# Three sets of four token tiles of the FFN's second layer as seven quarter products each; gates computed beside the first layer

## The chip, the cores and the metric

The kernel runs on one core of a Trainium2 chip. The metric is the time of one execution on the device in microseconds; 273.91 us is the median of 3 runs (273.66 to 274.04). All views below come from one execution, recorded by the hardware profiler (273.66 us).

The engines are named as the profile names them: PE (matrix products; PEld is its loading of the stationary operand), DVE (element-wise work), ACT (activations and copies out of PSUM), POOL (here the gathers and scatters of rows) and SP (which issues the loads of matrices). SBUF is the on-chip memory; PSUM holds the results of PE[...].

## The reference

Everything is fp32. There are 2048 tokens (4 x 512) of width 512.

```python
# first part: one of four experts for each token, chosen by its id
g = silu(einsum('bsd,fd->bsf', hidden_states, Wg[e]))      # Wg = Wu = Wd = ctx_2048
u = einsum('bsd,fd->bsf', hidden_states, Wu[e])
y = einsum('bsf,df->bsd', g * u, Wd[e])
out = where((expert_ids == e)[..., None], y, out)
x = x + tanh(g_xattn[0]) * out                             # hidden_states = layernorm(x)

# second part: a dense FFN, whose result is summed into 8 rows
route_probs = softmax(xr @ wr.T)                           # xr = layernorm(x)
routes_k, indices_k = top_k(route_probs, 2)
gates = routes_k / sum(routes_k)
h = silu(xr @ w1.T)
h = silu(h @ w3.T)
h = h @ w2.T
for k in range(2):
    out = out.at[indices_k[:, k]].add(gates[:, k:k+1] * h) # indices 0..7 are row numbers
x = x + tanh(g_ffn[0]) * out
```

The indices of the second part are row numbers of the output, so only rows 0 to 7 receive anything from the FFN. The kernel therefore sums the gated activations of all tokens into 8 rows before it multiplies by w2.

## The kernel before

The tokens are sorted by expert into 17 passes of 128 rows. A loop runs over the passes in a fixed `order`; iteration `i` issues, for different passes, `up` (product with the expert's matrix, line 537 or 522, into `z`), `turn_in`, `centre`, `look_at`, `gather`, `down` (second product, line 522, into `y`; line 571 adds it to the row), `load_free` (the next expert matrices), `turn_out` (transposed normed rows into `hT2`), `norms`, and then one or two `step()`s of the FFN. The order on each engine is the order in which the program issues (there is no scheduler): an instruction that waits holds up everything issued behind it on its engine.

The FFN works on two blocks `b` of 1024 tokens. `hT2[b]` holds a block's normed tokens, `s1` the first layer's output: 4 chunks of 128 features by 1024 tokens, of which columns 0 to 511 are "half 0" and 512 to 1023 "half 1". `ffn(b)` is a generator, and each `step()` runs it to its next `yield`. Block 0 starts in iteration 10 and its steps lie between the passes of iterations 11 to 18; block 1 starts in iteration 18 and has the chip to itself.

`first_layer` (lines 699 to 784) already forms the product with w1 by seven quarter products for eight (a 2 x 2 block product after Strassen and Winograd): products p1 to p7 out of sums `S1..S4` of quarters of w1 and `T1..T4` of quarters of `hT2`. X is a PSUM tile into which p1, p6, p5 and p3 are added one after the other, read in between by ACT (`kept`) or DVE (`active`).

`second_layer` forms the product with w3 in the plain way: `gated(t)` takes a tile of 128 tokens, four products of 128 x 128 by 128 x 512 into the PSUM tile `v` (line 824), and a Silu into `s2` (line 832). For each half of a block, 4 tiles; 16 in all. The very last tile is made in two halves of 256 columns. Then `add` multiplies `s2` by the gates `g` and sums it into four 32-row groups of `acc` (line 836); `pay` issues the adds of the half before. `route` (lines 623 to 667) finds the two largest logits and the gates on DVE, with one Tanh on ACT; it is issued in one piece ahead of each half's tiles.

Expert matrices are tiles of 1 MB in a pool of `MP = 7` buffers. `load_free` issues the load of unit `n` once the pass that last used unit `n - MP` has been issued in full:

```python
        while n < len(units) and (
            n < MP or max(order.index(p) for p in units[n - MP][0]) < i
        ):
            n += 1
```

A unit is one expert matrix; a pass with rows of all four experts has four of them, and neighbouring whole passes share one. Loads leave on SP's queue in the order of issue, w1, w3 and w2 among them. PSUM is divided into pools: `ps_mm` (2 banks: `z`, `y`, `Z`, `v`), `ps_x` (2: the logits and X), `ps_y` (1: Y), `ps_tp` (2: transposes), and one for `acc`. A tile of a pool takes over the bank of the second last one of that pool, and its first product waits until that one has been read.

Of the kernel before, what the change touches and what calls it, by code (L numbers as in the profile page):

```python
# [8 lines left out]
F32 = mybir.dt.float32  # L9
# [4 lines left out]
AF = mybir.ActivationFunctionType  # L14
# [5 lines left out]
P = 128  # L20
# [5 lines left out]
def tile_gated_moe_ffn(  # L26
# [45 lines left out]
    nc = tc.nc  # L72
# [15 lines left out]
    assert NB == 2 and KC == 4  # L88

    const = ctx.enter_context(tc.tile_pool(name="const", bufs=1))  # L90
    MP = 7
    mp = ctx.enter_context(tc.tile_pool(name="mp", bufs=MP))
    xp = ctx.enter_context(tc.tile_pool(name="xp", bufs=6))
    work = ctx.enter_context(tc.tile_pool(name="work", bufs=3))
# [528 lines left out]
    def route(b, lt):  # L623

        def st(name, shape=(P, TT, NR)):
            return small.tile(list(shape), F32, tag=name, name=f"{name}_{b}")

        def wide(a):
            return a.unsqueeze(2).to_broadcast([P, TT, NR])

        def first_max(src, i):
            mx = st(f"mx{i}", (P, TT))
            nc.vector.tensor_reduce(mx, src, AX.X, ALU.max)  # L640
            oh = st(f"oh{i}")
            nc.vector.tensor_tensor(oh, src, wide(mx), ALU.is_equal)
            nc.vector.tensor_mul(oh, oh, rank)
            rk = st(f"rk{i}", (P, TT))
            nc.vector.tensor_reduce(rk, oh, AX.X, ALU.max)
            nc.vector.tensor_tensor(oh, oh, wide(rk), ALU.is_equal)
            return mx, oh

        l1 = lt[:, :, 0:NR]
        m1, oh1 = first_max(l1, 1)  # L650
        l2 = st("l2")
        nc.vector.scalar_tensor_tensor(l2, oh1, -1e30, l1, ALU.mult, ALU.add)
        m2, oh2 = first_max(l2, 2)
        d = st("d", (P, TT))
        nc.vector.tensor_sub(d, m1, m2)
        half = st("half", (P, TT))
        nc.scalar.activation(half, d, AF.Tanh, scale=0.5)
        p1 = st("p1", (P, TT))
        nc.vector.tensor_scalar(p1, half, 0.5, 0.5, ALU.mult, ALU.add)
        p2 = st("p2", (P, TT))  # L660
        nc.vector.tensor_scalar(p2, half, -0.5, 0.5, ALU.mult, ALU.add)
        g = small.tile([P, TT, Q], F32, tag="g", bufs=2, name=f"g_{b}")
        nc.gpsimd.memset(g, 0.0)
        nc.vector.tensor_tensor(oh1, oh1, wide(p1), ALU.mult)
        nc.vector.tensor_tensor(oh2, oh2, wide(p2), ALU.mult)
        nc.vector.tensor_add(g[:, :, 0:NR], oh1, oh2)
        return g

    def sums_of_w1():

        h = D // 2
        a11, a12 = w1[:, 0:2, 0:h], w1[:, 2:4, 0:h]
        a21, a22 = w1[:, 0:2, h:D], w1[:, 2:4, h:D]
        ss = [ffp.tile([P, 2, h], F32, tag=f"S{i}", name=f"S{i}") for i in range(1, 5)]
        w1_sums.extend((a11, a12, a22, ss))
        nc.vector.tensor_add(ss[0], a21, a22)
        yield
        nc.vector.tensor_sub(ss[1], ss[0], a11)
        yield
        nc.vector.tensor_sub(ss[2], a11, a21)  # L680
        yield
        nc.vector.tensor_sub(ss[3], a12, ss[1])
        yield

    def sums_of_hT(b):


        lgs = [logits(b, half) for half in range(2)]
        b11, b12 = hT2[b][:, 0:2, 0:HB], hT2[b][:, 0:2, HB:TB]
        b21, b22 = hT2[b][:, 2:4, 0:HB], hT2[b][:, 2:4, HB:TB]  # L690
        ts = [ffp.tile([P, 2, HB], F32, tag=f"T{i}", name=f"T{i}_{b}") for i in range(1, 5)]
        nc.vector.tensor_sub(ts[0], b12, b11)
        lts[b] = [turned(b, half, lg) for half, lg in enumerate(lgs)]
        nc.vector.tensor_sub(ts[1], b22, ts[0])
        nc.vector.tensor_sub(ts[2], b22, b12)
        nc.vector.tensor_sub(ts[3], b21, ts[1])
        return b11, b21, b22, ts
# [108 lines left out]

    def ffn(b):

        yield from first_layer(b)
        for half in range(2):  # L810
            yield from second_layer(2 * b + half, route(2 * b + half, lts[b][half]))

    NH = 2 * NB

    def second_layer(b, g):

        c_b = b % 2 * HB

        def gated(t, half=None):

            c0, n = (0, D) if half is None else (half * D // 2, D // 2)
            v = ps_mm.tile([P, n], F32, tag="mm", name=f"v_{b}_{t}_{c0}")
            for k in range(KC):
                nc.tensor.matmul(  # L824
                    v,
                    s1[:, k, c_b + t * P : c_b + (t + 1) * P],
                    w3[:, k, c0 : c0 + n],
                    start=(k == 0),
                    stop=(k == KC - 1),
                )  # L830
            s2 = work.tile([P, n], F32, tag="s2", bufs=5, name=f"s2_{b}_{t}_{c0}")
            nc.scalar.activation(s2, v, AF.Silu)  # L832
            return s2

        def add(t, s2):
            nc.tensor.matmul(  # L836
                acc[t * Q : (t + 1) * Q, :],
                g[:, t, :],
                s2,
                start=(b == 0),  # L840
                stop=(b == NH - 1 if t < TT - 2 else b == NH - 2),
            )

        def pay():

            for f, t, s2 in owed:
                f(t, s2)
            owed.clear()

        def add_turned(t, k, s2):  # L850

            nc.tensor.matmul(  # L852
                accT[:, k, :],
                s2,
                g[:, t, 0:NR],
                start=(t == TT - 2 and k == 0),
                stop=(t == TT - 1 and k == KC - 1),
                skip_group_check=True,
            )

        s2s = []
        if b < NH - 1:
            for t in range(TT):
                s2s.append(gated(t))
                if t == 0:
                    pay()
                yield
            owed.extend((add, t, s2s[t]) for t in range(TT))
            return
        for t in range(TT - 1):  # L870
            s2s.append(gated(t))
            if t == 0:
                pay()
            yield
        for t in range(TT - 2):
            add(t, s2s[t])
        a = work.tile([P, D], F32, tag="g", bufs=1, name="a")
        nc.scalar.copy(a, acc)
        half0 = gated(TT - 1, 0)
        for k in range(KC):  # L880
            add_turned(TT - 2, k, s2s[TT - 2][:, k * P : (k + 1) * P])
        tp = transposed(a, "sum")
        nc.vector.tensor_reduce(
            aT[:, :, 0:NR],
            tp.rearrange("p (k t q) -> p k q t", k=KC, t=TT)[:, :, 0:NR, :],
            AX.X,
            ALU.add,
        )
        def finish(i, s2):
            n = KC // 2  # L890
            for k in range(n):
                add_turned(TT - 1, i * n + k, s2[:, k * P : (k + 1) * P])
            ks = slice(i * n, (i + 1) * n)
            nc.vector.tensor_add(aT[:, ks, 0:NR], aT[:, ks, 0:NR], accT[:, ks, :])

        finish(0, half0)
        half1 = gated(TT - 1, 1)
        out_product(0, KC // 2)
        finish(1, half1)

    o = []
# [15 lines left out]

    SHORT = 1
    last = {b: max(i for i, p in enumerate(order) if min(p // (TB // P), NB - 1) == b) for b in range(NB)}
    running, hT_sums, lts, w1_sums = [], {}, {}, []  # L920

    def step():
        if running:
# [52 lines left out]
    turn_mid(order[1])  # L976
    norms(order[4], order[0])
    summing = sums_of_w1()
    owed = []
    for i in range(2, NP + 2):  # L980
        if i < NP:
            up(order[i])
        if i + 1 < NP:
            turn_in(order[i + 1])
        if i + 2 < NP:
            centre(order[i + 2])
        if i + 3 < NP:
            look_at(order[i + 3])
        if i + 4 < NP:
            gather(order[i + 4])  # L990
        if i <= NP:
            down(order[i - 1])
        load_free(i)
        turn_out(order[i - 2])
        if i <= NP:
            norms(order[i + 3] if i + 3 < NP else None, order[i - 1])
        step()
        if i > NP:
            step()
        if 6 <= i < 10:  # L1000
            next(summing)
        if i == 4:
            w1 = load_w(w1T, "w1")
            wr = load_w(wrT, "wr")
        if i == 8:
            w3 = load_w(w3T, "w3")
        if i == 12:
            w2 = load_w(w2T, "w2")
        if i < NP:
            turn_mid(order[i])  # L1010
        for b in range(NB):
            if last[b] == i - 2:
                hT_sums[b] = sums_of_hT(b)
                running.append(ffn(b))
        if last[0] != i - 2:
            step()
# [53 lines left out]
```

## Time and profile before

| what | value |
|---|---|
| median of 3 runs (lowest, highest) | 273.91 us (273.66, 274.04) |
| profiled execution: its time | 273.66 us |
| profiled execution: span from first to last instruction | 271.9 us |
| PE busy | 264.2 us, 1383 products |
| DVE, ACT, POOL busy | 146.5, 63.5, 39.1 us |
| granted clock of PE, mean | 0.997 |
| line 824 (`v`) on the chain that ended last | 20% of the span |
| bytes moved | 37.32 MB, mean 137 GB/s |

The span leaves out 1.76 us of the profiled execution's time, which lie around it. An fp32 product of the program appears as two loads of the stationary operand and two MATMUL records, so one tile of `gated` is 8 records. Records overlap (each is longer than the distance to the next), so what a product costs is read from the distance between starts or from the chain of waits, not from the mean length of a record. The chain of waits lists, in order of time, what had to end before the next thing could start; a line of it is the start, the length, the engine and the tile.

### The profile page before, as it was taken

The page shows a single profiled execution, that of the slowest core. Times are in us where ns is not written, and L with a number is a line of the kernel's source. Part 1 is how long each engine was busy: PE and PEld are TensorE (multiplying, and loading weights), DVE is VectorE, ACT ScalarE, POOL GpSimd, SP SyncE. Part 2 cuts the span into 40 slices and gives each one's busy share as a digit, 9 for nine tenths or more (in the row PEclk, how much of TensorE's full clock was granted, in tenths as well). Part 3 has the DMA queues.
Part 4 walks back from the last instruction along what each step waited for, and adds up shares of the span by engine and source line. Part 5 has one row for each costly group of instructions (what it writes and reads, how often), then busy time and mean ns, then how long its engine had stood idle before and what let it go on. Part 6 is the DMA issues. An engine that isn't in the chain of part 4 may idle for free.

```text
span 271.9 us, 3831 instructions
## 1 busy us (share of the span) xinstructions
PE 264.2 (97%) x1383; PEld 142.2 (52%) x1383; DVE 146.5 (54%) x498; ACT 63.5 (23%) x124; POOL 39.1 (14%) x61
## 2 busy tenths in 40 slices
PE   5999999999999999999999999999999999999994
PEld 2545484757783757435746534464445444344363
DVE  6697986864888989936263471417244521701000
ACT  2013232122222121233041231211122233301120
POOL 5440122211222320311010100101010000000000
PEclk9999999999999999999999999999999999999998
DMA  0666994499974459915429510100010000000000
GB/s 1 236 193 257 387 393 172 140 303 377 367 275 168 155 155 375 350 42 162 185 75 386 194 39 2 39 0 10 2 41 0 0 2 0 0 0 0 0 2 4
DMA packets 18083, 37.32 MB, mean 137 GB/s; under 512 B 2063, under 2 KB 2127, under 8 KB 18064
## 3 DMA queue, kind: packets, MB, share of 16 engines
q1 hardware_dynamic: 15312, 28.41, 29.6%
q0 software_dynamic: 2720, 8.65, 8.8%
q8 instruction: 11, 0.18, 0.3%
q14 instruction: 8, 0.07, 0.1%
q10 hardware_dynamic: 32, 0.01, 0.0%
HBM read 32.86 MB, written 4.47 MB: 137 GB/s over the span
## 4 chain that ended last, share of the span: by engine, by line
PE 96%; DMA 2%; DVE 1%; issue 0%; DVEq 0%
PE y L522 22%; PE v L824 20%; PE z L537 13%; PE X L716 10%; PE z L522 9%; PE Y L716 5%; PE tp_f L407 3%; PE tp_a L407 3%; PE Z L716 3%; PE idle L212 2%; PE acc L836 1%; PE lg L793 1%; DMA x<-in_x_dram,from_row 1%; PE tp_g L407 1%; PE accT L852 1%; DMA idt<-in_ids_dram 1%
## 5 line engine op out<-in xcount | busy, mean ns | idle before, releaser
L824 PE MATMUL v<-w,s 128*128 128x512 f32 (+1 forms) x136 | 57.2, 570 | 0.0
L824 PEld LDWEIGHTS v<-w,s 128*128 128x128 f32 x136 | 25.1, 190 | 28.2 <-issue 27.1
L537 PEld LDWEIGHTS z<-hT,m 128*128 128x128 f32 x320 | 36.8, 192 | 1.6 <-issue 1.4
L537 PE MATMUL z<-hT,m 128*128 128x128 f32 x320 | 37.5, 275 | 0.0
L522 PE MATMUL y<-m,g 128*128 128x512 f32 x80 | 36.1, 594 | 0.0
L572 POOL DMA_INDIRECT out_dram<-x,to_row x17 | 17.2, 1009 | 90.8 <-DVE x L571 89.0
L522 PE MATMUL z<-m,hT 128*32 128x512 f32 (+1 forms) x152 | 25.7, 596 | 0.6 <-DVE hT L471 0.6
L522 PE MATMUL y<-m,gT 128*32 128x512 f32 (+1 forms) x152 | 25.4, 595 | 0.0
L418 POOL DMA_INDIRECT x<-in_x_dram,rows_on x14 | 14.4, 1027 | 63.0 <-DVE x L571 19.6
L522 PEld LDWEIGHTS y<-m,g 128*128 128x128 f32 x80 | 14.4, 190 | 15.2 <-issue 15.2
L571 DVE SCALAR_TENSOR_TENSOR x<-y,tg,x 128x512 f32<-128x512 f32 x17 | 12.6, 740 | 17.7 <-PE y L522 17.7
L555 DVE TENSOR_TENSOR g<-z,g 128x512 f32<-128x512 f32 x14 | 9.6, 688 | 22.0 <-ACT g L554 22.0
L554 ACT ACTIVATE g<-z 128x512 f32<-128x512 f32 x14 | 8.4, 598 | 48.3 <-PE z L537 36.1
L832 ACT ACTIVATE s<-v 128x512 f32<-128x512 f32 (+1 forms) x17 | 9.7, 571 | 42.2 <-PE v L824 42.2
L609 ACT COPY hT<-tp_f 128x512 f32<-128x512 f32 x13 | 7.6, 586 | 39.9 <-PE tp_f L407 39.9
L372 DVE BATCH_NORM_STATS2 st_a<-x 128x6 f32<-128x512 f32 x17 | 11.7, 686 | 6.6 <-DMA x<-in_x_dram,rows_on 6.6
L522 PEld LDWEIGHTS z<-m,hT 128*32 128x32 f32 (+1 forms) x152 | 7.9, 122 | 13.8 <-issue 10.6
L716 PE MATMUL X<-T,S 128*128 128x512 f32 x32 | 15.0, 592 | 0.0
L522 PEld LDWEIGHTS y<-m,gT 128*32 128x32 f32 (+1 forms) x152 | 8.1, 122 | 12.1 <-issue 12.0
L407 PEld LDWEIGHTS tp_f<-ident,h_f 128*128 128x128 f32 x68 | 8.2, 141 | 10.2 <-issue 10.2
L372 DVE BATCH_NORM_STATS2 st_f<-x 128x6 f32<-128x512 f32 x17 | 11.8, 694 | 0.6
L734 DVE TENSOR_TENSOR s<-X,c 128x512 f32<-128x512 f32 x4 | 2.8, 691 | 15.0 <-PE X L716 15.0
(183 smaller groups left out, 284.3 us busy)
## 6 DMA issues: line engine op xcount, KB each, us to landing
m<-in_ctxT_dram SPq DMA_DIRECT2D x24, 1024.0 KB
w<-in_w1T_dram SPq DMA_DIRECT2D x1, 1024.0 KB
w<-in_w3T_dram SPq DMA_DIRECT2D x1, 1024.0 KB
w<-in_w2T_dram SPq DMA_DIRECT2D x1, 1024.0 KB
out_dram<-x,to_row POOLq DMA_INDIRECT x17, 5.6
x<-in_x_dram,rows_on POOLq DMA_INDIRECT x14, 6.0
wr<-in_wrT_dram SPq DMA_DIRECT2D x1, 64.0 KB
x_first<-out_dram SPq DMA_DIRECT2D x4, 4.0 KB
```

What stands on the lines that cost most here:

```text
L372: nc.vector.bn_stats(st, xt)
L407: nc.tensor.transpose(tp[:, k * P : (k + 1) * P], h[:, k * P : (k + 1) * P], ident)
L418: nc.gpsimd.indirect_dma_start(out=xt, out_offset=None, in_=x, in_offset=bass.IndirectOffsetOnAxis(ap=from_row0 if p == order[0] else (fro ...
L522: nc.tensor.matmul(out_ps[i * n : (i + 1) * n, :], lhs[:, k * P + i * n : k * P + (i + 1) * n], m[:, k, :], start=(k == 0), stop=(k == KC ...
L537: nc.tensor.matmul(z[:, c * P : (c + 1) * P], mats[p][0][:, k, c * P : (c + 1) * P], hT[:, k * P : (k + 1) * P], start=(k == 0), stop=(k = ...
L554: nc.scalar.activation(g, z, AF.Silu)
L555: nc.vector.tensor_mul(g, z, g)
L571: nc.vector.scalar_tensor_tensor(xt, y, tg[:, 0:1], xt, ALU.mult, ALU.add)
L572: nc.gpsimd.indirect_dma_start(out=out, out_offset=bass.IndirectOffsetOnAxis(ap=to_row[:, p : p + 1], axis=0), in_=xt, in_offset=None, bou ...
L716: nc.tensor.matmul(out_ps, a[:, k, c * P : (c + 1) * P], bb[:, k, :], start=start and k == 0, stop=k == 1, skip_group_check=True,)
L824: nc.tensor.matmul(v, s1[:, k, c_b + t * P : c_b + (t + 1) * P], w3[:, k, c0 : c0 + n], start=(k == 0), stop=(k == KC - 1),)
L832: nc.scalar.activation(s2, v, AF.Silu)
```

## The change

Twelve of the sixteen tiles (block 0 whole, and tiles 0 and 1 of both halves of block 1) are no longer made by `gated`. `coupled(b, c0)` makes four tiles at a time: tiles `c0` and `c0 + 1` of half 0 and of half 1. In the terms of its 2 x 2 block product, the left matrix has the tokens of half 0 and half 1 as its rows and the features 0 to 255 and 256 to 511 as its columns, and w3 is cut into four quarters. Seven products for each of the two tile pairs, each of two 128 x 128 by 128 x 256 products, take the place of sixteen 128 x 128 by 128 x 512 ones. The sums of `s1` quarters (`A1`, `A2`, a third in place in `s1`, `A4`) are made on DVE for each set, the sums of w3 (`V1..V4`) once, in iterations 10 to 13. X, Z and Y hold partial results; ACT copies three of them for each tile pair, DVE adds them. A set has four `yield`s, as four tiles had, so the number of steps does not change. The last four tiles of block 1 are made as before (`last_tiles`).

`route` is cut into three pieces by two `yield`s, and both halves of a block are routed during the last steps of its first layer. `pay` for the last set of block 0 is issued in the first layer of block 1. `MP` goes from 7 to 6, the third sum of w1 is written over a quarter of w1 and the third sum of `hT2` over a quarter of `hT2`.

```diff
--- before.py
+++ after.py
@@ -88,7 +88,7 @@
     assert NB == 2 and KC == 4
 
     const = ctx.enter_context(tc.tile_pool(name="const", bufs=1))
-    MP = 7
+    MP = 6
     mp = ctx.enter_context(tc.tile_pool(name="mp", bufs=MP))
     xp = ctx.enter_context(tc.tile_pool(name="xp", bufs=6))
     work = ctx.enter_context(tc.tile_pool(name="work", bufs=3))
@@ -653,13 +653,15 @@
         m2, oh2 = first_max(l2, 2)
         d = st("d", (P, TT))
         nc.vector.tensor_sub(d, m1, m2)
+        yield
         half = st("half", (P, TT))
         nc.scalar.activation(half, d, AF.Tanh, scale=0.5)
+        yield
         p1 = st("p1", (P, TT))
         nc.vector.tensor_scalar(p1, half, 0.5, 0.5, ALU.mult, ALU.add)
         p2 = st("p2", (P, TT))
         nc.vector.tensor_scalar(p2, half, -0.5, 0.5, ALU.mult, ALU.add)
-        g = small.tile([P, TT, Q], F32, tag="g", bufs=2, name=f"g_{b}")
+        g = small.tile([P, TT, Q], F32, tag="g", bufs=4, name=f"g_{b}")
         nc.gpsimd.memset(g, 0.0)
         nc.vector.tensor_tensor(oh1, oh1, wide(p1), ALU.mult)
         nc.vector.tensor_tensor(oh2, oh2, wide(p2), ALU.mult)
@@ -671,7 +673,8 @@
         h = D // 2
         a11, a12 = w1[:, 0:2, 0:h], w1[:, 2:4, 0:h]
         a21, a22 = w1[:, 0:2, h:D], w1[:, 2:4, h:D]
-        ss = [ffp.tile([P, 2, h], F32, tag=f"S{i}", name=f"S{i}") for i in range(1, 5)]
+        ss = [ffp.tile([P, 2, h], F32, tag=f"S{i}", name=f"S{i}") for i in (1, 2, 4)]
+        ss.insert(2, a21)
         w1_sums.extend((a11, a12, a22, ss))
         nc.vector.tensor_add(ss[0], a21, a22)
         yield
@@ -680,6 +683,22 @@
         nc.vector.tensor_sub(ss[2], a11, a21)
         yield
         nc.vector.tensor_sub(ss[3], a12, ss[1])
+        yield
+
+    def sums_of_w3():
+
+        h = D // 2
+        b11, b12 = w3[:, 0:2, 0:h], w3[:, 0:2, h:D]
+        b21, b22 = w3[:, 2:4, 0:h], w3[:, 2:4, h:D]
+        ts = [ffp.tile([P, 2, h], F32, tag=f"V{i}", name=f"V{i}") for i in range(1, 5)]
+        w3_sums.extend((b11, b21, b22, ts))
+        nc.vector.tensor_sub(ts[0], b12, b11)
+        yield
+        nc.vector.tensor_sub(ts[1], b22, ts[0])
+        yield
+        nc.vector.tensor_sub(ts[2], b22, b12)
+        yield
+        nc.vector.tensor_sub(ts[3], b21, ts[1])
         yield
 
     def sums_of_hT(b):
@@ -688,7 +707,8 @@
         lgs = [logits(b, half) for half in range(2)]
         b11, b12 = hT2[b][:, 0:2, 0:HB], hT2[b][:, 0:2, HB:TB]
         b21, b22 = hT2[b][:, 2:4, 0:HB], hT2[b][:, 2:4, HB:TB]
-        ts = [ffp.tile([P, 2, HB], F32, tag=f"T{i}", name=f"T{i}_{b}") for i in range(1, 5)]
+        ts = [ffp.tile([P, 2, HB], F32, tag=f"T{i}", name=f"T{i}_{b}") for i in (1, 2, 4)]
+        ts.insert(2, b12)
         nc.vector.tensor_sub(ts[0], b12, b11)
         lts[b] = [turned(b, half, lg) for half, lg in enumerate(lgs)]
         nc.vector.tensor_sub(ts[1], b22, ts[0])
@@ -806,46 +826,153 @@
 
     def ffn(b):
 
-        yield from first_layer(b)
-        for half in range(2):
-            yield from second_layer(2 * b + half, route(2 * b + half, lts[b][half]))
-
-    NH = 2 * NB
-
-    def second_layer(b, g):
-
-        c_b = b % 2 * HB
-
-        def gated(t, half=None):
-
-            c0, n = (0, D) if half is None else (half * D // 2, D // 2)
-            v = ps_mm.tile([P, n], F32, tag="mm", name=f"v_{b}_{t}_{c0}")
-            for k in range(KC):
+        gs_ = []
+
+        def routes():
+            for half in range(2):
+                gs_.append((yield from route(2 * b + half, lts[b][half])))
+
+        looking = routes()
+        for i, _ in enumerate(first_layer(b)):
+            if i == 1:
+                pay()
+            if i > 1:
+                next(looking, None)
+            yield
+        yield from coupled(b, 0, gs_)
+        if b < NB - 1:
+            yield from coupled(b, 2, gs_)
+        else:
+            yield from last_tiles(b, gs_)
+
+    def gated(b, half, t, part=None):
+
+        c0, n = (0, D) if part is None else (part * D // 2, D // 2)
+        v = ps_mm.tile([P, n], F32, tag="mm", name=f"v_{b}_{half}_{t}_{c0}")
+        for k in range(KC):
+            nc.tensor.matmul(
+                v,
+                s1[:, k, half * HB + t * P : half * HB + (t + 1) * P],
+                w3[:, k, c0 : c0 + n],
+                start=(k == 0),
+                stop=(k == KC - 1),
+            )
+        s2 = work.tile([P, n], F32, tag="s2", bufs=5, name=f"s2_{b}_{half}_{t}_{c0}")
+        nc.scalar.activation(s2, v, AF.Silu)
+        return s2
+
+    def add(i, g, t, s2, start, stop):
+
+        nc.tensor.matmul(
+            acc[i * Q : (i + 1) * Q, :],
+            g[:, t, :],
+            s2,
+            start=start,
+            stop=stop,
+            skip_group_check=True,
+        )
+
+    def pay():
+
+        for a in owed:
+            add(*a)
+        owed.clear()
+
+    def coupled(b, c0, gs_):
+
+        n = D // 2
+        b11, b21, b22, (t1, t2, t3, t4) = w3_sums
+        cs = (c0, c0 + 1)
+        a11s, a12s, a22s, sums = [], [], [], []
+        for c in cs:
+            lo, hi = slice(c * P, (c + 1) * P), slice(HB + c * P, HB + (c + 1) * P)
+            a11, a12, a21, a22 = s1[:, 0:2, lo], s1[:, 2:4, lo], s1[:, 0:2, hi], s1[:, 2:4, hi]
+            sa = [
+                ffp.tile([P, 2, P], F32, tag=f"A{i}", bufs=2, name=f"A{i}_{b}_{c}")
+                for i in (1, 2, 4)
+            ]
+            nc.vector.tensor_add(sa[0], a21, a22)
+            nc.vector.tensor_sub(sa[1], sa[0], a11)
+            sa.insert(2, a21)
+            a11s.append(a11), a12s.append(a12), a22s.append(a22), sums.append(sa)
+
+        for sa, a11, a12 in zip(sums, a11s, a12s):
+            nc.vector.tensor_sub(sa[2], a11, sa[2])
+            nc.vector.tensor_sub(sa[3], a12, sa[1])
+
+        def product(to, a, bb, start):
+            for k in range(2):
                 nc.tensor.matmul(
-                    v,
-                    s1[:, k, c_b + t * P : c_b + (t + 1) * P],
-                    w3[:, k, c0 : c0 + n],
-                    start=(k == 0),
-                    stop=(k == KC - 1),
+                    to,
+                    a[:, k, :],
+                    bb[:, k, :],
+                    start=start and k == 0,
+                    stop=k == 1,
+                    skip_group_check=True,
                 )
-            s2 = work.tile([P, n], F32, tag="s2", bufs=5, name=f"s2_{b}_{t}_{c0}")
-            nc.scalar.activation(s2, v, AF.Silu)
-            return s2
-
-        def add(t, s2):
-            nc.tensor.matmul(
-                acc[t * Q : (t + 1) * Q, :],
-                g[:, t, :],
-                s2,
-                start=(b == 0),
-                stop=(b == NH - 1 if t < TT - 2 else b == NH - 2),
-            )
-
-        def pay():
-
-            for f, t, s2 in owed:
-                f(t, s2)
-            owed.clear()
+
+        def keep_(name):
+            return ffp.tile([P, 2, n], F32, tag=name, name=f"{name}_{b}_{c0}_v")
+
+        def s2_tiles(half):
+            return [
+                work.tile([P, D], F32, tag="s2", bufs=5, name=f"s2_{b}_{half}_{c}") for c in cs
+            ]
+
+        xs_ = []
+        c1 = keep_("c1")
+        for i in range(2):
+            xs_.append(ps_x.tile([P, n], F32, tag="x", name=f"X_{b}_{cs[i]}_v"))
+            product(xs_[i], a11s[i], b11, True)
+            nc.scalar.copy(c1[:, i, :], xs_[i])
+        pay()
+        lows = s2_tiles(0)
+        z = ps_mm.tile([P, 2, n], F32, tag="mm", name=f"Z_{b}_{c0}_v")
+        for i in range(2):
+            product(z[:, i, :], a12s[i], b21, i == 0)
+        for i in range(2):
+            nc.vector.tensor_add(lows[i][:, 0:n], z[:, i, :], c1[:, i, :])
+        yield
+        u2, c7 = keep_("u2"), keep_("c7")
+        for i in range(2):
+            product(xs_[i], sums[i][1], t2, False)
+            nc.scalar.copy(u2[:, i, :], xs_[i])
+        y = ps_y.tile([P, 2, n], F32, tag="y", name=f"Y_{b}_{c0}_v")
+        for i in range(2):
+            product(y[:, i, :], sums[i][2], t3, i == 0)
+        nc.scalar.copy(c7, y)
+        for i in range(2):
+            nc.scalar.activation(lows[i][:, 0:n], lows[i][:, 0:n], AF.Silu)
+        yield
+        highs = s2_tiles(1)
+        for i in range(2):
+            product(xs_[i], sums[i][0], t1, False)
+            nc.vector.tensor_add(highs[i][:, n:D], xs_[i], c7[:, i, :])
+        for i in range(2):
+            product(y[:, i, :], a22s[i], t4, False)
+        for i in range(2):
+            nc.vector.tensor_add(highs[i][:, 0:n], y[:, i, :], u2[:, i, :])
+        yield
+        for i in range(2):
+            product(xs_[i], sums[i][3], b22, False)
+            nc.scalar.activation(lows[i][:, n:D], xs_[i], AF.Silu)
+        for i in range(2):
+            nc.scalar.activation(highs[i], highs[i], AF.Silu)
+        first_, last_ = b == 0 and c0 == 0, b == NB - 1
+        owed.extend((i, gs_[0], cs[i], lows[i], first_, False) for i in range(2))
+        owed.extend((2 + i, gs_[1], cs[i], highs[i], first_, last_) for i in range(2))
+        yield
+
+    def last_tiles(b, gs_):
+
+        g = gs_[1]
 
         def add_turned(t, k, s2):
 
@@ -858,27 +985,20 @@
                 skip_group_check=True,
             )
 
-        s2s = []
-        if b < NH - 1:
-            for t in range(TT):
-                s2s.append(gated(t))
-                if t == 0:
-                    pay()
-                yield
-            owed.extend((add, t, s2s[t]) for t in range(TT))
-            return
-        for t in range(TT - 1):
-            s2s.append(gated(t))
-            if t == 0:
-                pay()
-            yield
-        for t in range(TT - 2):
-            add(t, s2s[t])
+        s2s = [gated(b, 0, TT - 2)]
+        pay()
+        yield
+        s2s.append(gated(b, 0, TT - 1))
+        yield
+        s2s.append(gated(b, 1, TT - 2))
+        yield
+        for i in range(2):
+            add(i, gs_[0], TT - 2 + i, s2s[i], False, True)
         a = work.tile([P, D], F32, tag="g", bufs=1, name="a")
         nc.scalar.copy(a, acc)
-        half0 = gated(TT - 1, 0)
+        half0 = gated(b, 1, TT - 1, 0)
         for k in range(KC):
-            add_turned(TT - 2, k, s2s[TT - 2][:, k * P : (k + 1) * P])
+            add_turned(TT - 2, k, s2s[2][:, k * P : (k + 1) * P])
         tp = transposed(a, "sum")
         nc.vector.tensor_reduce(
             aT[:, :, 0:NR],
@@ -886,6 +1006,7 @@
             AX.X,
             ALU.add,
         )
+
         def finish(i, s2):
             n = KC // 2
             for k in range(n):
@@ -894,7 +1015,7 @@
             nc.vector.tensor_add(aT[:, ks, 0:NR], aT[:, ks, 0:NR], accT[:, ks, :])
 
         finish(0, half0)
-        half1 = gated(TT - 1, 1)
+        half1 = gated(b, 1, TT - 1, 1)
         out_product(0, KC // 2)
         finish(1, half1)
 
@@ -917,7 +1038,7 @@
 
     SHORT = 1
     last = {b: max(i for i, p in enumerate(order) if min(p // (TB // P), NB - 1) == b) for b in range(NB)}
-    running, hT_sums, lts, w1_sums = [], {}, {}, []
+    running, hT_sums, lts, w1_sums, w3_sums = [], {}, {}, [], []
 
     def step():
         if running:
@@ -976,6 +1097,7 @@
     turn_mid(order[1])
     norms(order[4], order[0])
     summing = sums_of_w1()
+    summing3 = sums_of_w3()
     owed = []
     for i in range(2, NP + 2):
         if i < NP:
@@ -999,6 +1121,8 @@
             step()
         if 6 <= i < 10:
             next(summing)
+        if 10 <= i < 14:
+            next(summing3)
         if i == 4:
             w1 = load_w(w1T, "w1")
             wr = load_w(wrT, "wr")

```

## The prediction

> **What bounds the kernel now.** I read the page first (busy shares, slices, chain), then the waits of PE, then the chain in order of time, then the stretches around the FFN on DVE, ACT and SP.
>
> ```profile
> PE 264.2 (97%) x1383; PEld 142.2 (52%) x1383; DVE 146.5 (54%) x498; ACT 63.5 (23%) x124; POOL 39.1 (14%) x61
> PE   5999999999999999999999999999999999999994
> PEclk9999999999999999999999999999999999999998
> PE 96%; DMA 2%; DVE 1%; issue 0%; DVEq 0%
> ```
>
> PE is busy in all slices but the first and the last, at full granted clock, and it is 96% of the chain. The waits of PE, complete:
>
> ```profile
> PE cnt L205 <- DVE hot L202: 2.9, 1, 2.9
> PE z L522 <- DVE hT L471: 0.6, 1, 0.6
> PE tp_a L462 <- DMA x<-in_x_dram,from_row: 0.4, 1, 0.4
> PE o L908 <- DVE aT L894: 0.3, 1, 0.3
> ```
>
> From 23 us to the last product for row 0, PE never waits. So in the stretch that the change touches, a microsecond of PE taken out is a microsecond of the end, as long as nothing else becomes late. The chain shows what the replaced tiles cost:
>
> ```profile
> 196.81 6.87 PE v L824 x16
> ...
> 231.95 1.72 PE X L716 x4
> 233.67 3.43 PE v L824 x8
> 237.10 1.00 PE acc L836 x8
> 238.10 13.93 PE v L824 x32
> ```
>
> Two tiles in 6.87, one in 3.43: 0.429 us a record of 512 columns, 13.74 us for four tiles. (The 13.93 holds 0.19 that a tile pays after `acc`; there are as many `pay`s after the change as before, so this stays.)
>
> **Part 1: the products.** A set has 7 products x 2 tile pairs x 2 chunks x 2 records = 56 records of 256 columns, for 4 x 8 = 32 records of 512. The trace has 256-column records of the same operands, in the two halves of the last tile. Asked in stretches of a quarter microsecond, their starts are (first column):
>
> ```profile
> 264.78 0.81 PE L824 MATMUL v<-w,s 128*128 128x256 f32 x3
> ...
> 266.07 0.38 PE L824 MATMUL v<-w,s 128*128 128x256 f32 x1
> ```
>
> Six steps lie between these two starts (those between them are at 265.00, 265.21, 265.43, 265.64 and one more): 0.215 us each, half of 0.429. A set is 56 x 0.215 = 12.04 us; it saves 13.74 - 12.04 = 1.70, and three sets 5.1 us.
>
> A rule of the Trainium skill speaks against this. There are 56 loads of the stationary operand in a set where there were 32, and a load has a mean of 190 ns:
>
> ```profile
> L537 PE MATMUL z<-hT,m 128*128 128x128 f32 x320 | 37.5, 275 | 0.0
> L537 PEld LDWEIGHTS z<-hT,m 128*128 128x128 f32 x320 | 36.8, 192 | 1.6 <-issue 1.4 <-DVE r_f L391 0.2
> L824 PEld LDWEIGHTS v<-w,s 128*128 128x128 f32 x136 | 25.1, 190 | 28.2 <-issue 27.1 <-DVE q_f L385 0.5 <-DVE q_f L399 0.2
> 147.07 3.57 PE z L537 x32
> ```
>
> "TensorE: Matmul & The Clock Gate", Part 3, What overlaps and what doesn't, says that a load runs beside running products only where it goes to another row group, which these full 128-row loads never do. By it the 24 more loads of a set add 24 x 0.19 = 4.6 us, and the change would lose 4.6 - 1.7 = 2.9 us a set, 8.6 in all. The row disagrees: 32 records of 128 columns take 3.57 us, 0.112 each, less than the 0.19 of the load that each has. The loads are hidden at 128 columns already, so at 256 they are. I take the row; the sum stays 5.1.
>
> **Part 2: DVE.** New for each set: 8 sums over 256 columns. 512 columns take 684 ns, 1024 take 1214, so 1.04 ns a column: about 0.42 for 256, and 0.34 from start to start, since rows of one queue overlap by 0.08. That is 2.8 us. Six adds out of PSUM at about 0.42: 2.5. Once, four sums of w3 at 0.60 from start to start: 2.4. Together 18 us of DVE. None is on the path unless PE waits for it, and I looked for where:
> - Iteration 10, `V1`. It goes ahead of the `T` sums, and DVE runs without a gap from there to the first add out of Z, which frees the bank that `z` of iteration 12 takes:
>
> ```profile
> 115.28 0.68 DVE L734 TENSOR_TENSOR s<-Z,c 128x512 f32<-128x512 f32 x1
> 116.69 3.57 PE z L522 x32
> ```
>
>   The add ends at 115.96, with `V1` at 116.56; `z` starts at 116.69 and takes some 0.05 to see it (line 894 to the last `o`: 267.81 to 267.86). It just fits; 0 to 0.1 us.
> - Sets 1 and 2, between passes. DVE in set 1 is free at about 160.0 (norms, the last add of the first layer, the last piece of the gates at 0.8 us), the sums end at 162.8, the adds out of Z at 163.6; the bank is taken by `y` at 165.97. p6 of the set comes a whole pass later. Nothing.
> - Set 3 has nothing between its products. PE enters it at the time that was 233.67. The sums need the Silu of p3 (ACT, to 234.31) and start there; the two that p6 reads end at about 235.1 and 235.8, and PE reaches p6 at 233.67 + 3.44 = 237.1. The third and fourth sums are done by 237.2, when PE needs them from 238.8 on. Nothing.
>
> **Part 3: ACT.** For each set four copies of 256 (375 ns), one of 512 (586), four Silus of 256 (384) and two of 512 (600): 4.8 us for the 2.4 of four Silus. The close place is the second X of a set, which takes the bank that the last p3 of the first layer left to its Silu:
>
> ```profile
> 233.71 0.60 ACT L737 ACTIVATE s<-X 128x512 f32<-128x512 f32 x1 [2.01 <-PE X L716]
> ```
>
> It is read out at 234.31, and the second X starts one product pair after 233.67, at 234.53. Between sets 1 and 2 the Silu is of 256 columns, and there is more room. The adds of set 1 in set 2 need the last Silu of `highs` about 1.5 us after p3, and come 1.72 after it. The copy out of Y (0.59) has the two p5 pairs (1.72) before p4 writes Y again. I count 0 for ACT and 0.1 us for all such places together.
>
> **Part 4: the gates.** The same instructions, about 3.6 us of DVE and 0.2 of ACT for each half, move from ahead of the tiles into iterations 12 to 14 (block 0) and into the first layer of block 1. DVE has gaps of 1.5 to 3.5 us there (130.4, 136.3, 147.2); the adds out of X and Y that they delay by up to 3 us are next missed by p3 at 140.2 and p7 at 143.6. POOL's four memsets (0.23 us each) no longer wait for `acc`, and sit behind scatters that are issued anyway. Cost 0; no gain either, since PE never waited for the gates.
>
> **Part 5: six buffers.** With `MP` 6, SP issues units later. I went through the rule of `load_free` for all 24. The tight ones are the four of the pass at 116.69 (three of them now go out at 99.3, with one for a later pass, as many bytes as before at that point; the transfers of that batch ended at about 114.5) and the four of the pass at 161.82:
>
> ```profile
> 139.62 3.18 SPq L501 DMA_DIRECT2D m<-in_ctxT_dram  x4
> ```
>
> All four now leave here (before it was three of these and one later unit); what left here ended at 153, 9 us ahead. The single unit for 147.07 leaves at 124.3, the last one at 154.5 for 177.15. w3 no longer queues behind a unit's load on SP, leaves at the same 75.4, and is wanted at 104. Cost 0. If 2.2 us of that cover at 116.69 were gone, the rest of the delay would stand on the path in full.
>
> **The sum.** -5.1 + 0.1 = -5.0 us. Against the profiled execution: span 271.9 to 266.9, time 273.66 to 268.7. The median of the runs lies 0.25 above that execution; 273.91 - 5.0 = 268.9.
>
> **Rivals.**
> - A, as summed: 268.9, with 268.4 to 269.4 for the small places.
> - B, the hand-overs miss: sets are finer grained than tiles, with a hand-over from ACT or DVE to PE every 0.86 us. If some four of them (`z` at 116.69, the second X in sets 1 and 3, the adds in set 2) cost 0.3 us each, 1.2 comes back: 270.1. For it: the margins of 0.1 to 0.2 us. Against it: `first_layer` has the same pattern, and PE's list of waits has no entry from it.
> - C, slower: the sums in place. A third sum is written over columns of half 1 of two chunks of `s1`, and the next products read half 0 of the same chunks. In memory the write is two strips with a strip of half 0 between them. `v` at 233.67 starts while ACT still writes another strip of `s1` (line 737, 233.71), so waits go by address and not by tile; but those strips are in one piece each. If the program's waits are drawn by the range that encloses the two strips, the first X would wait for the last third sum: from 158.8 to 162.5 in set 1 (3.7), 186.6 to 190.9 in set 2 (4.3), 234.1 to 236.8 in set 3 (2.7), and the `T3` in place holds p1 of block 1 from 210.3 to 212.1 (1.8). That is 12.5 lost for 5.0 won: 281.4. It decides as soon as these waits pass 5.0 together, two of the sets with the `T3` wait. No row of this trace shows a write in strips beside a read; I hold it unlikely, since a wait per strip is as easily drawn.
> - D, loads not hidden at 256 columns in this mixture: by the rule above 273.9 + 8.6 = 282.5. The 0.215 steps speak against it.
> - E, no change: PE's saving is taken up by a pass that waits for its matrices in the loop (Part 5) and by B. 273.9.
>
> **Chances.** A 0.80, B 0.12, C 0.04, D 0.01, E 0.03. A and B hold 0.92; the range takes A's and B's places, 268.3 to 270.3. About 0.2% (0.55 us) is what a measurement of this kernel can tell from no change: faster 0.93, same 0.02, slower 0.05.
>
> **What the profile after should show.** PE busy near 259, still over 96% of the span, with no wait of over 0.3 us from 23 us on. In the chain, set 3 takes 12.0 us between the last X of `first_layer` and the first `v`; its records step by 0.215. DVE busy near 164, ACT near 71. `z` of iteration 12 starts at about 116.7 and `z` of iteration 15 at 161.8 as now, and the end of the loop comes 3.4 earlier. I am wrong if PE shows waits for DVE in the sets (C), if records of 256 step by more than 0.23 (D), or if a pass starts after a DMA (E).

## The result and the profile after

The changed kernel takes 268.91 us (median of 4 runs, 268.86 to 268.95) for 273.87 (4 runs, 273.66 to 274.04) of the kernel before on the same chip: a ratio of 0.9819 (95% interval 0.9802 to 0.9836), 4.96 us less. 268.9 was predicted. The profiled execution has a span of 267.2 us for 271.9.

The page of the changed kernel, busy time, slices and chain:

```profile
PE 259.4 (97%) x1455; PEld 155.7 (58%) x1455; DVE 163.9 (61%) x544; ACT 69.4 (26%) x145; POOL 38.7 (14%) x61
PE   5999999999999999999999999999999999999994
PEclk9999999999999999999999999999999999999999
PE 96%; DMA 2%; DVE 1%; issue 0%; DVEq 0%
```

PE lost 4.8 us of work and is as full as before. DVE gained 17.4 us of work and ACT 5.9, and PE shows no new wait for them: its waits are the same four, of the same lengths.

```profile
PE cnt L205 <- DVE hot L202: 2.9, 1, 2.9
PE z L522 <- DVE hT L471: 0.6, 1, 0.6
PE tp_a L462 <- DMA x<-in_x_dram,from_row: 0.4, 1, 0.4
PE o L1029 <- DVE aT L1015: 0.3, 1, 0.3
```

The chain of the changed kernel at the passes whose matrices or banks (a bank is the piece of PSUM that one tile holds) were close to being late, and through the third set:

```profile
116.73 3.57 PE z L522 x32
...
158.42 1.82 PE X_v L911 x8
160.23 1.73 PE Z_v L911 x8
161.96 3.57 PE z L522 x32
...
231.70 1.82 PE X_v L911 x8
233.51 1.73 PE Z_v L911 x8
235.24 1.73 PE X_v L911 x8
236.97 1.73 PE Y_v L911 x8
238.69 1.73 PE X_v L911 x8
240.42 1.73 PE Y_v L911 x8
242.15 1.73 PE X_v L911 x8
243.87 3.43 PE v L853 x8
```

A pair of products (8 records of 256 columns) takes 1.73, 0.216 a record; set 3 takes 243.87 - 231.70 = 12.17 us for 13.74. With 12.20 for set 1 and 12.1 for set 2 (its pieces of the chain, without the 0.19 after `acc`) the three sets take 36.5 for 41.2: 4.7, which is the difference of the spans. Whatever else changed moved the end by less than 0.1.

In sets 1 and 3 the first piece reads 1.82, not 1.73. The timeline of the changed kernel shows a cause (start, length, engine, and in brackets the idle time ahead and what ended it):

```profile
231.73 0.60 ACT L757 ACTIVATE s<-X 128x512 f32<-128x512 f32 x1 [2.01 <-PE X L736]
232.38 0.73 PEld L911 LDWEIGHTS X_v<-w,s 128*128 128x128 f32 x4 [0.23 <-ACT s L757]
233.96 0.42 DVE L906 TENSOR_TENSOR s<-s 128x256 f32<-128x256 f32 x1
```

The load for the second X comes 0.05 after ACT has read the bank (231.73 + 0.60 = 232.33), and 0.23 after the load before it ended. This is a hand-over: PE waits for what another engine has still to finish. A run below takes it away. The last line is for rival C: the first sum in place is written from 233.96 on, when the first X products, which read the strip beside it, were done (their piece ends at 233.51). They did not wait for it.

### The profile page after: what moved, and what is told of

It reads as the page before. It is cut to its first block, busy times and chain, and to the rows that moved or that the text cites. A ratio compares the mean times of both kernels' runs of the same rounds, so it can differ in the third digit from the quotient of the medians.

```text
span 267.2 us, 4056 instructions
## 1 busy us (share of the span) xinstructions
PE 259.4 (97%) x1455; PEld 155.7 (58%) x1455; DVE 163.9 (61%) x544; ACT 69.4 (26%) x145; POOL 38.7 (14%) x61
## 4 chain that ended last, share of the span: by engine, by line
PE 96%; DMA 2%; DVE 1%; issue 0%; DVEq 0%
PE y L522 22%; PE z L537 13%; PE X L736 10%; PE z L522 9%; PE X_v L911 8%; PE v L853 5%; PE Y L736 5%; PE Y_v L911 4%; PE tp_f L407 3%; PE tp_a L407 3%; PE Z L736 3%; PE Z_v L911 2%; PE idle L212 2%; PE acc L866 1%; PE lg L813 1%; DMA x<-in_x_dram,from_row 1%
## 5 line engine op out<-in xcount | busy, mean ns | idle before, releaser
L522 PEld LDWEIGHTS y<-m,gT 128*32 128x32 f32 (+1 forms) x152 | 8.1, 122 | 12.1 <-issue 12.0
L853 PE MATMUL v<-w,s 128*128 128x512 f32 (+1 forms) x40 | 14.7, 514 | 0.0
L911 PE MATMUL X_v<-V,A 128*128 128x256 f32 x48 | 11.4, 379 | 0.0
L911 PE MATMUL Y_v<-V,s 128*128 128x256 f32 x48 | 11.3, 379 | 0.0
L853 PEld LDWEIGHTS v<-w,s 128*128 128x128 f32 x40 | 7.4, 190 | 6.8 <-issue 6.5
```

The source lines that it names most:

```text
L522: nc.tensor.matmul(out_ps[i * n : (i + 1) * n, :], lhs[:, k * P + i * n : k * P + (i + 1) * n], m[:, k, :], start=(k == 0), stop=(k == KC ...
L853: nc.tensor.matmul(v, s1[:, k, half * HB + t * P : half * HB + (t + 1) * P], w3[:, k, c0 : c0 + n], start=(k == 0), stop=(k == KC - 1),)
L911: nc.tensor.matmul(to, a[:, k, :], bb[:, k, :], start=start and k == 0, stop=k == 1, skip_group_check=True,)
```

## The experiments

Theory 1: the gain is the columns that PE no longer streams, and all else in the change is free because something covers it. Rivals: the gates out of the way brought part of it (theory 2); the sixth buffer's loss took something back (theory 3); loads of the stationary operand are not hidden (D). "Covers" is meant in time: a cover is how long a result is ready before PE asks for it.

The changed kernel was timed beside a kernel before of 273.87 us. On the chips of the runs below, but for the last two, the kernel before takes 273.71 or 273.77, so a difference to the 268.91 of the changed kernel may hold some 0.2 us that belong to the chip.

### The gates alone

Only the part of the edit in `ffn` is shown; with it go the two `yield`s in `route`, `routes()` as in the changed kernel and four buffers for the gates.

```diff
-        yield from first_layer(b)
-        for half in range(2):
-            yield from second_layer(2 * b + half, route(2 * b + half, lts[b][half]))
+        looking = routes()
+        for i, _ in enumerate(first_layer(b)):
+            if i > 1:
+                next(looking, None)
+            yield
+        for half in range(2):
+            yield from second_layer(2 * b + half, gs_[half])
```

> The kernel before with one part of the change: route in three pieces, both halves of a block routed during its first layer, four buffers for the gates. All 16 tiles stay plain. Theory 1 (the gain is PE's columns and nothing else): DVE and ACT work is moved that PE never waited for, so 273.9, within 0.3. Theory 2 (part of the gain is that the gates no longer stand ahead of the tiles): faster than before by 0.5 or more, 273.4 or less, and the three coupled sets are worth that much less.

273.72 us for 273.71 (ratio 0.9998, 0.9989 to 1.0007). Theory 2, which asked for 0.5 or more, falls: to move the gates neither wins nor costs anything over 0.3 us, which is as far as the interval reaches.

### Six buffers alone

```diff
-    MP = 7
+    MP = 6
```

> The kernel before with MP = 6 in place of 7 and nothing else. Theory 1: every pass still finds its matrices, PE shows no wait for a transfer, 273.9 within 0.3. Theory 3 (the sixth buffer's loss costs something that the products pay for): slower, 274.4 or more, with a PE wait for a DMA at the passes that started at 116.69 or 161.82.

273.82 for 273.71 (1.0007, 1.0 to 1.0015): at most 0.4 us, and PE has no wait for a transfer of a matrix. Its chain has the passes where the kernel before has them (116.69, 147.07, 161.82), 0.03 earlier:

```profile
116.66 3.57 PE z L522 x32
...
147.04 3.57 PE z L537 x32
161.79 3.57 PE z L522 x32
```

SP's own view shows what the buffer did: five loads now start in the stretch that held four, and the last of them, for which a buffer comes free only then, is issued by 154.9, ahead of its pass at 177.13.

```profile
139.59 15.29 SPq L501 DMA_DIRECT2D m<-in_ctxT_dram  x5
```

### Two sets in place of three

```diff
-        yield from coupled(b, 0, gs_)
         if b < NB - 1:
+            yield from coupled(b, 0, gs_)
             yield from coupled(b, 2, gs_)
         else:
+            plain = []
+            for half in range(2):
+                for t in range(2):
+                    plain.append((2 * half + t, gs_[half], t, gated(b, half, t), False, half == 1))
+                    yield
+            owed.extend(plain)
             yield from last_tiles(b, gs_)
```

> The changed kernel with its third set (tiles 0 and 1 of both halves of block 1) made as four plain tiles again. Theory 1: the set that took 12.17 us (231.70 to 243.87) takes 4 x 3.435 = 13.74, so 268.9 + 1.57 = 270.5. If the gain came from elsewhere (gates, owed adds), the time stays within 0.5 of 268.9; if the three sets share 4.95 unevenly because sets 1 and 2 hide a wait, the step differs from 1.6 by over 0.4.

270.73, that is 1.8 above the changed kernel; the spans differ by 1.6 (268.8 and 267.2), and the chain of this kernel has five plain tiles in one piece:

```profile
231.74 17.17 PE v L859 x40
```

17.17 for the 12.17 + 3.43 of the changed kernel is 1.57, as expected. The third set is worth a third of the 4.7.

### Twice as many loads

The edit, with the arguments shortened:

```diff
             for k in range(2):
-                nc.tensor.matmul(to, a[:, k, :], bb[:, k, :], ...)
+                for h in range(2):
+                    nc.tensor.matmul(
+                        to[:, h * P : (h + 1) * P], a[:, k, :], bb[:, k, h * P : (h + 1) * P], ...)
```

> The changed kernel with every 256-column product of the three sets cut into two of 128 columns, so that 168 records become 336 and each loads its stationary operand again. Theory 1 (loads are hidden down to 128 columns): 0.1116 a record as in z of line 537, so 168 x (0.2232 - 0.2164) = 1.1 more, 270.0. Rival D (a load of 0.19 is not hidden beside a full product): 168 more loads of 0.19, 32 us more, 300.9. In between, loads hidden at 256 but bound by 0.19 at 128: 336 x 0.19 - 36.4 = 27.4 more.

270.2, 1.3 above the changed kernel. Two pieces of its chain, in set 3:

```profile
236.17 1.79 PE X_v L912 x16
237.95 1.79 PE Y_v L912 x16
```

16 records of 128 columns take 1.79, 0.112 each, and each has a load of its own of 0.19, as the sum over one kind of product shows (records, busy time in us, mean in ns):

```profile
L912 PEld LDWEIGHTS X_v<-V,A 128*128 128x128 f32 x96 | 11.2, 192 | 0.0
```

96 loads of 0.192 make 18.4 us and fill only 11.2, so the loads overlap each other too. Rival D falls. For these fp32 products the rule of the Trainium skill that was weighed in the prediction ("TensorE: Matmul & The Clock Gate", Part 3, What overlaps and what doesn't) does not hold as it is put there: with 168 more loads that nothing hides this kernel would, by the estimate above, take 301.

### More sums ahead of p6

```diff
-            nc.vector.tensor_add(sa[0], a21, a22)
-            nc.vector.tensor_sub(sa[1], sa[0], a11)
+            for _ in range(3 if b == NB - 1 else 1):
+                nc.vector.tensor_add(sa[0], a21, a22)
+                nc.vector.tensor_sub(sa[1], sa[0], a11)
```

> The changed kernel with the first two sums of the third set written three times over, for each of its two tile pairs: 8 more DVE operations ahead of p6, nothing else. In the changed kernel's trace the two sums of the first pair are ready at 233.24 and of the second at 234.04, while p6 loads them at 234.86 and about 235.7. Theory 1 with a cover: a pair of sums takes 0.80 from start to start, so the second pair's come at 232.36 + 6 x 0.80 = 237.2, 1.5 us after PE wants them: 268.9 + 1.5 = 270.4, with a PE wait for DVE at line 911. If DVE were never on the path, whatever it does: 268.9. If the added work itself counted: 3.2 more, 272.1.

271.21, 2.3 above the changed kernel, where 1.5 was expected. The wait is the one that was named, p6 of the second pair for that pair's sum:

```profile
PE X_v L912 <- DVE A L902: 1.5, 1, 1.5
```

```profile
233.92 0.42 DVE L902 TENSOR_TENSOR A<-A,s 128x256 f32<-128x256 f32 x1
234.38 0.43 DVE L901 TENSOR_TENSOR A<-s 128x256 f32<-128x256 f32 x1
234.84 0.42 DVE L902 TENSOR_TENSOR A<-A,s 128x256 f32<-128x256 f32 x1
...
238.04 1.10 PE X_v L912 x4
```

The sums step by 0.46, not by 0.40 on average. The changed kernel has both steps: a sum that needs the one before starts 0.46 after it, and one that does not, 0.34 to 0.35.

```profile
232.36 0.43 DVE L900 TENSOR_TENSOR A<-s 128x256 f32<-128x256 f32 x1 [0.95 <-ACT s L757]
232.82 0.42 DVE L901 TENSOR_TENSOR A<-A,s 128x256 f32<-128x256 f32 x1
233.17 0.42 DVE L900 TENSOR_TENSOR A<-s 128x256 f32<-128x256 f32 x1
```

In the run nearly every sum reads what the one before wrote, or writes over what it read, so the last one ends at 237.89, 0.7 later than I had it. In the chain set 3 takes 14.2 us (231.89 to 246.05) for 12.17, 2.0 more: 1.8 at the second p6 and 0.2 at the first, whose sum was repeated too (the 1.5 of the wait list counts only PE's idle time). The rest of the 2.3 is the start of this execution, which lies 0.2 later from the first products on. So DVE is on the path once its cover of 1.6 us is used up, and 8 sums too many use it up. "Free" in theory 1 is a matter of this cover.

### p3 ahead of p4 in the first layer

```diff
-            (p4, 0), (p3, 0), (p6, 1), (p7, 1), (p5, 1), (p4, 1), (p3, 1),
+            (p4, 0), (p3, 0), (p6, 1), (p7, 1), (p5, 1), (p3, 1), (p4, 1),
```

> The changed kernel with p3 and p4 of the first layer's second pair in the other order. The first X product of sets 1 and 3 took 1.82 in place of 1.73; the load for the second X ends an idle time of 0.23 that ACT's Silu of p3 ended. If that hand-over is the cause, both pieces fall to 1.73 and the time by 0.18, to 268.7, since the Silu is done 1.7 us earlier; the sums then start some 0.8 later, within their cover of 1.6. If the 0.09 belongs to the change from 512 to 256 columns, nothing changes: 268.9.

269.95: 1.0 slower. The hand-over was what I said it was; in this kernel's chain both first pieces fall to 1.73:

```profile
158.35 1.73 PE X_v L911 x8
...
226.39 1.73 PE X L736 x4
...
228.21 0.70 DVE s L754
...
230.94 1.72 PE Y L736 x4
232.66 1.73 PE X_v L911 x8
```

But p3 adds into the X that p5 has just filled, and DVE must read it in between. With p4 between them PE had 1.72 of other work; without it, in block 1, it waits:

```profile
228.96 1.98 PE L736 MATMUL X<-hT,S 128*128 128x512 f32 x4 [0.85 <-DVE s L754]
```

p4 (the Y at 230.94), issued behind p3 and with all that it reads ready, starts only after it. I had looked at who waits for p3's Silu and not at what p3 waits for. In block 0 a pass lies between p5 and p3, and there is no such wait. In the chain p5 and p3 of block 1 take 4.55 (226.39 to 230.94) for 3.44, so 0.18 was won and 1.1 lost.

### A fourth set, alone and with the other order

The edit, cut short: its first lines and, as comments, the order that the last set then has.

```diff
-            yield from last_tiles(b, gs_)
+            yield from coupled(b, 2, gs_)      # for both blocks; from p5 on, in the last set:
+        # p5, p5, p3, p3, p4(0), the two adds of half 0, copy of acc, p4(1), its transposes,
+        # then both tiles of half 1 turned into two PSUM banks, and the product with w2
```

> The changed kernel with the last four tiles as a fourth set as well. From p5 on it has its own order: p3 ahead of p4, the adds of half 0 between the two p4, the two Y in banks of their own, and the transposed sums of half 1 in two banks. Theory 1: 13.74 + 0.2 (two halves in place of one tile) become 12.1, 1.8 less; the tail has one DVE wait less and two half products fewer between, some 0.4: 268.9 - 2.2 = 266.7. Rival: the plain last tiles are there because their Silu and sums hide beside the last products; a set ends with an add and a Silu more after its last product (0.42 + 0.38 and the hand-overs, about 1 us) for both tiles, and the tail takes back what the products save: 268.5 to 269.5.

> The fourth set and the other order of p3 and p4 together. If both are as theory 1 has them, 0.18 under the kernel with four sets alone: about 266.5.

267.29 (266.94 to 267.72) alone, ratio 0.9767 (0.9751 to 0.9784): faster than the changed kernel, whose interval begins at 0.9802. The end of its chain:

```profile
252.31 3.45 PE X_v L989 x16
255.76 0.86 PE Yy_v L989 x4
256.62 0.98 PE acc L863 x4
257.61 1.06 PE Ymm_v L989 x4
258.67 0.44 PE tp_sum L407 x4
259.11 0.79 PE accT L1026 x8
259.90 0.89 PE accT_lo L1026 x8
260.79 1.05 PE o L1051 x32
261.87 0.35 DVE ob L1174
```

The last element-wise step starts at 261.87 where the changed kernel has 263.85: 2.0 earlier, although this execution's first set starts 0.3 later; from the first set on it is 2.3, for the 2.2 expected. The rival's tail did not come: the Silu of the last quarter (259.17 to 259.59) hides beside the transposes and the turned sums of the other three quarters (258.67 to 259.90). The median is only 1.6 below the changed kernel's: the four executions lie 0.8 apart, and the profiled one is the fastest of them. With the other order of p3 and p4 it is 267.79, and PE waits again as in the run before:

```profile
PE X L736 <- DVE s L754: 0.9, 1, 0.9
```

### Four sets, the other order in block 0 only

The edit is shown against the kernel with four sets.

```diff
+        if b == 0:
+            todo[-2:] = [(p3, 1), (p4, 1)]
```

> Four sets, with p3 ahead of p4 in block 0 only. In e6 the other order took the first X product from 1.82 to 1.73 in both sets, but in block 1, where p3 then follows p5 directly, it waited 0.9 for DVE to read X. In block 0 a pass stands between p5 and p3. If that is all, the time is 0.09 under that of four sets alone (267.2 for 267.3), which the runs can hardly tell, and the first X product of set 1 shows 1.73 with no new wait of PE. If the order costs in block 0 too (the sums start later and the bank of Z with them), a wait of PE for DVE shows there and the time is above 267.3.

> Four sets alone once more, on the same chip as the run beside it: 267.3, as before (266.9 to 267.7).

These two ran on a chip where the kernel before takes 274.8 (274.04 to 275.23). With the other order in block 0: 267.75 (267.21 to 269.43); four sets alone: 267.33 (267.28 to 268.18). The times do not tell the two apart; the chains do. First with the other order, then without it, the first X piece of set 1 and the last element-wise step:

```profile
159.41 1.73 PE X_v L910 x8
...
262.44 0.35 DVE ob L1176
```

```profile
159.97 1.82 PE X_v L908 x8
...
263.09 0.35 DVE ob L1174
```

From the one step to the other it is 103.03 us with the other order, for 103.12 without it (103.12 in the earlier run of that kernel too). The hand-over is gone where it was meant to go, the end comes 0.09 earlier, and PE has no wait that it does not have without the other order. Four sets alone have a ratio of 0.9732 (0.9714 to 0.9749) here; with 267.29 and 267.33 they have the lowest medians of the study.

## Why the prediction was right, point by point

- **What bounds.** Right. PE was 97% busy before and after, and the spans differ by what the sets lost. The loop ends 3.2 earlier (204.39 for 207.56), for the 3.4 forecast.
- **Part 1, the products.** Right in kind and nearly in size: 1.57 for set 3 by the run with two sets, for 1.70. A record of 256 columns takes 0.216 in a set, for the 0.215 of the last tile's halves; over 168 records this is 0.2 us.
- **Loads.** To take the row and not the rule was the right choice, and the run with twice the loads shows it.
- **Part 2, DVE.** 17.4 us of new work for the 18 counted. `z` of iteration 12 starts at 116.73 for 116.69, in an execution that is 0.04 later from its first row gather on, so the margin of 0.1 held. In set 3 the sums began at 232.36, 0.66 after the set, as worked out. Their cover was 1.6, not the 2.0 that was worked out (235.1 to 237.1): the load of p6 comes ahead of its product (234.86 for 235.24 in the chain), and a sum that needs the one before steps by 0.46, not 0.34. The run with more sums used this cover up.
- **Part 3, ACT.** The mis-sized term. The second X was given 0.22 of room, reckoned from the end of the Silu to the start of the product. What has to be in time is the product's load, a fifth of a microsecond ahead of it (in set 3 the first load for Z starts at 233.14, its product at 233.35). The hand-over costs 0.09 in set 1 and 0.09 in set 3, 0.18 where 0.1 was set down for all such places; it goes where the Silu comes earlier. Of the four places of rival B these two cost something, at 0.09 each for 0.3, so 0.18 came back for its 1.2.
- **Parts 4 and 5.** Nothing that the runs can tell: the gates alone lie between 0.3 faster and 0.2 slower, six buffers alone between 0 and 0.4 slower, and neither has a new wait of PE. The `pay` that moves into the first layer of block 1 was not run alone; on the chain it takes 1.00 (at 213.34), as each `pay` did before.
- **The sum.** -4.7 in the span for -5.0: 0.2 from the records and 0.1 from the hand-overs. That the median still came out at 268.91 for 268.9 is in part luck: the medians differ by 4.96 and the profiled spans by 4.7. The quarter microsecond between them is less than the executions of the kernel before differ from each other (273.66 to 274.04).
- **Rivals C and E.** C fell because the third sum of set 3 started after the products that it would have held, and PE shows no wait for DVE in any set; a third sum in a tile of its own was not run. E fell because no pass waits for a transfer.

## What to carry to other kernels

Where PE is full from end to end, seven products for eight are worth nearly one eighth of the time of the products they replace (here 4.7 of 41.2 us). What decides is whether 256-column products keep their price a column (here 0.216 us a record for 0.429 at 512) and whether each added element-wise step has its cover. Count a cover from the moment at which the consumer's load is issued, not from its product. Before you reorder two products to help one hand-over, list what each of them waits for itself.

## What had not been expected of the hardware

Two DVE sums of 256 fp32 columns start 0.34 us apart when they are independent and 0.46 when the second needs the first, with the same 0.42 of busy time; here a chain of such sums is a third slower than its count says. Why is not shown. Loads of 0.19 us stay hidden beside 128-column products of 0.112, and their records overlap (96 of 0.192 us in 11.2).
